# Where the score scatters are issued in a two-layer graph kernel: held back around each batch's features

## The chip, the cores and the metric

The kernel runs on one core of one Trainium2 chip. The metric is the device time of one execution in microseconds (us); for a kernel, the median of several runs. TensorE is written PE, VectorE DVE, ScalarE ACT, GpSimd POOL and SyncE SP, as the profile does. Each engine works through a queue of its own in the order in which the program was written down, and waits on semaphores.

## What is computed

Inputs are `x` (16 batches x 1024 nodes x 256) and one 1024 x 1024 matrix `adj` that is mostly zero (the edge lists below have room for 135 x 128 entries). Two graph layers follow each other for every batch:

```python
# layer 0
feats  = x @ W1.T;  f1 = feats @ W2 + b2
coefs  = softmax(leaky_relu(f1[:, None] + f1[None, :]) + adj)
h      = coefs @ feats + bias2 + x
# layer 1
S      = sigmoid(relu(h[u] @ W1u + h[v] @ W1v + b1) @ W2 + b2)   # for each pair u, v
a      = (S * adj).T @ h
m      = (adj @ h) * h
z      = beta1*h + beta2*(a @ Wa + ba) + beta3*(m @ Wm + bm)
```

`S` is multiplied by `adj`, so it matters only where `adj` has an edge.

## The kernel before

**Layer 0, batch by batch.** For each of 16 batches PE makes the features from the turned `x` (`begin_features`, four steps of 4 matmuls each, L991), then the row of f (`begin_f`: eight transposes at L965), and then attention in eight chunks (`attention(b, c)`, 8 matmuls of 128 x 257 each, L1041); each matmul of these two lines shows as two instructions in the profile. The features and the row of f of batch b + 1 are written down right after attention chunk 7 of batch b. Each features step needs one of two PSUM buffers of pool `p2`. It is emptied by DVE, which clips two columns (L1004, tile `f`), and then by ACT, which takes their exponential (L1008) and scales the features with it (L1016); only after that may PE fill the buffer again. Two further chains end at the same spot: attention's rows are divided and added by DVE (`keep_h`, L1052 and L1055), and the row of f is reduced by DVE (L973) and turned into `row` and `col` by ACT (L979, L980, L984), from which DVE spreads the weights of the next attention (L1028).

**Layer 1, edge by edge.** After attention, `h` is projected to both ends of an edge (`end`, L1079) and stored to memory. The scores are made on lists of edges, for three groups of batches together (5, 5 and 6 batches). A list has 135 slots for each group; a slot is 128 edges, and one slot is one *round*. In a round
- POOL fetches the far ends for the slot three rounds ahead (`fetch`, an indirect DMA, L1200 into tile `gv`, one of five buffers) and in every eighth round or so the near ends too (L1193, tile `gu`),
- DVE takes the maximum and minimum of the two ends (`compare`, two instructions of L1229),
- ACT adds up, one instruction pair for each batch of the group (`sums`, L1243); in a quarter of the last group's rounds DVE does it instead (L1240),
- after 16 rounds (a *part*) ACT applies tanh (`gates`, L1251), DVE adds one (L1270), and the part's 16 results are appended to the list `late` as 16 *scatters*: indirect DMAs of POOL, one for each slot (L1209, `sa_d<-lg,idx_s`).

The scatters are not issued at once. At the start of each round, behind its fetch, the function `first` takes one of them from `late`, or two when more than 12 stand there (`PARTS[0] - 4`). What is left at the end of the last group is issued together. Fetches and scatters stand in one queue, POOL's, in the order written down.

**What sets the order.** A `Timetable` holds entries of a planned time and a function; `run()` sorts them by time and calls them, so the planned time decides the order on every engine's queue and nothing else. `times.now` is moved along by PE's planned work. The rounds of a group are spread evenly between two planned times by `scores(g, start, end, ...)`: a round every 3.67 us in the first group (planned 391 to 879), 3.47 in the second (883 to 1348) and 3.86 in the third (1351 to 1868). `scores` is called when the whole loop over the batches has been written down. Rounds of the first two groups therefore lie beside layer 0 of batches 5 to 15, the third beside the products and `gather` of groups already scored (L1139, L1159, L1344); there ACT and DVE prepare the gathers' weights (tile `apart`, L1326 and L1331) from `sat`, loaded by SP.

Of the kernel before, what the change touches and what calls it, by code (L numbers as in the profile page):

```python
# [371 lines left out]
def edge_layers(  # L372
# [59 lines left out]
    first = first_stack.enter_context(tc.tile_pool(name="first", bufs=1, side="right"))  # L432
# [750 lines left out]
    PARTS = [16, 32, 48, 64, 80, 96, 112, 124, 131, len(SLOTS)]  # L1183
    AHEAD = GV - 2
    HA = 9
    SA = 7
    late = []

    def fetch(g, k):
        t, s = SLOTS[k]  # L1190
        if s == 0:
            gu = st["gu", t] = pools["gath", g].tile([P, SIZE[g] * R], F32, name="gu", bufs=2)
            nc.gpsimd.indirect_dma_start(  # L1193
                out=gu,
                out_offset=None,
                in_=pu_d[g],
                in_offset=bass.IndirectOffsetOnAxis(ap=key_u[:, t : t + 1], axis=0),
            )
        gv = st["gv", k] = pools["gath", g].tile([P, SIZE[g] * R], F32, name="gv", bufs=GV)
        nc.gpsimd.indirect_dma_start(  # L1200
            out=gv,
            out_offset=None,
            in_=pw_d[g],
            in_offset=bass.IndirectOffsetOnAxis(ap=idx_v[:, t, s : s + 1], axis=0),
        )

    def scatter(g, lg, i, k):
        t, s = SLOTS[k]
        dma = nc.gpsimd.indirect_dma_start(  # L1209
            out=sa_d[g],  # L1210
            out_offset=bass.IndirectOffsetOnAxis(ap=idx_s[:, t, s : s + 1], axis=0),
            in_=lg[:, i, : SIZE[g]],
            in_offset=None,
            bounds_check=N * N - 1,
            oob_is_err=False,
        )
        tc.declare_no_dep(dma.ins, group=f"sa{g}", reason="edges of their own")
        tc.add_to_no_dep_group(f"sa{g}", dma.ins)
# [12 lines left out]
    def place_of(k):  # L1231

        part = next(i for i, end in enumerate(PARTS) if k < end)
        return (PARTS[part - 1] if part else 0), PARTS[part]
# [18 lines left out]
    def scores(g, start, end, on_vector):  # L1253

        for k in range(len(SLOTS)):
            time = start + k * (end - start) / len(SLOTS)

            def first(k=k):
                for n in range(AHEAD) if k == 0 else ():
                    fetch(g, n)  # L1260
                if k + AHEAD < len(SLOTS):
                    fetch(g, k + AHEAD)
                for _ in range(min(len(late), 2 if len(late) > PARTS[0] - 4 else 1)):
                    late.pop(0)()

            def last(k=k):
                k0, k1 = place_of(k)
                lg = st["lg", k0]
                part = lg[:, : k1 - k0, : SIZE[g]]
                nc.vector.tensor_scalar(part, part, 1.0, None, ALU.add)  # L1270
                late.extend(lambda i=i: scatter(g, lg, i, k0 + i) for i in range(k1 - k0))

            times.at(time - (15.0 if k == 0 else 0.0), first)
            times.at(time + 0.1, lambda k=k: compare(k, 0))
            times.at(time + 0.9, lambda k=k: compare(k, 1))
            k0, k1 = place_of(k)
            if k == k0:
                times.at(time + 0.2, lambda k0=k0: st.update({("lg", k0): st["lg"]}))
            summed = lambda js, k=k, k0=k0: sums(k, js, st["lg", k0])
            if on_vector(k):  # L1280
                times.at(time + 1.7, lambda f=summed: f(range(SIZE[g])))
            else:
                for j in range(SIZE[g]):
                    times.at(time + 2.0 + 0.6 * j, lambda f=summed, j=j: f((j,)))
            if k + 1 == k1:
                times.at(time + 5.4, lambda k=k, k0=k0: gates(g, k, st["lg", k0]))
                times.at(time + 6.0, last)
        ended = end + 4.0
        if g + 1 == NG:
            times.at(ended, lambda: [late.pop(0)() for _ in range(len(late))])  # L1290
        return ended
# [118 lines left out]
    def attention(b, c):  # L1410
        end = times.matmuls(C * (D + 1), lambda: attend(b, c))
        times.at(end + 0.6, lambda: keep_h(b, c))
# [29 lines left out]
    times = Timetable()  # L1442
# [23 lines left out]
    for b in range(B):  # L1466
        at_once = b > 0 and b - 1 not in LATER
        more = b + 1 < B

        if b:  # L1470
            weigh_ends(b - 1, 2)
            one_end(b - 1, 2, 1)
            if at_once:
                messages(b - 1, 0, 0)
            one_end(b - 1, 3, 0)
            one_end(b - 1, 3, 1)
            weigh_ends(b - 1, 3)
            if b - 1 in LATER:
                times.at(times.now, lambda b=b: put_off(b - 1))
            if any(b == lo for lo, _ in GROUPS):  # L1480
                started.append(times.now + 19.0)
        attention(b, 0)
        if b == 0:
            grows(6, 7)
        if at_once:
            messages(b - 1, 0, 1)
        attention(b, 1)
        spreads(b, 0)
        if more:
            times.at(times.now, lambda b=b: load_x(b + 1))  # L1490
        if at_once:
            products(b - 1, 0, 1)
        if b == 0:
            for i in range(2):
                for h in range(H):
                    times.matmuls(2 * R, lambda i=i, h=h: sort_columns(i, h))
            times.matmuls(2 * R, sort_bias)
        attention(b, 2)
        if at_once:
            messages(b - 1, 1, 0)  # L1500
        turned_ends(b, 0)
        attention(b, 3)
        spreads(b, 1)
        if at_once:
            messages(b - 1, 1, 1)
        both_ends(b, 0)
        attention(b, 4)
        if at_once:
            products(b - 1, 2, 3)
        if not more:  # L1510
            times.at(times.now, lambda: take_up(LATER[0]))
            times.at(times.now + 20.0, lambda: take_up(LATER[1]))
        turned_ends(b, 1)
        if more:
            begin(b + 1, 0)
        attention(b, 5)
        both_ends(b, 1)
        if more:
            begin(b + 1, 1)
        attention(b, 6)  # L1520
        turned_ends(b, 2)
        attention(b, 7)
        for c2 in range(C // 2):
            if more:
                begin_features(b + 1, c2)
        one_end(b, 2, 0)
        turned_ends(b, 3)
        if more:
            begin_f(b + 1)
# [58 lines left out]
    b = B - 1  # L1588
    for n in range(3):
# [4 lines left out]
        time = products(b, 2, 3)  # L1594
        b = LATER[n]
# [31 lines left out]
    for i, at in starts.items():  # L1627
        if i == 5:
            continue
        b = LATER[i]  # L1630
# [53 lines left out]
    for n, (g, c) in enumerate((g, c) for g in order for c in range(C)):  # L1684
# [4 lines left out]
        else:  # L1689
            k, c1 = divmod(n - HA, C)  # L1690
# [77 lines left out]
```

## Time and profile before

| what | value |
|---|---|
| median of 3 runs | 2165.57 us (2164.74 to 2166.67) |
| the profiled execution's own time | 2166.46 us |
| its span, first to last instruction | 2164.4 us |
| PE busy | 2054.0 us (95%) |
| DVE, ACT, POOL busy | 1565.5, 1378.6, 1128.4 us |
| scatters L1209 | 405, 496.1 us of POOL |
| fetches L1200 | 405, 481.1 us of POOL |
| granted clock of PE, mean | 0.985 |
| first fetch and first scatter begin | 376.8 and 454.8 us |
| last scatter issued, last group's gathers follow | 1975.2 us |

All of it is one execution; times in the views count from its first instruction, and 2.06 us of its 2166.46 lie outside the span. Busy time is an engine's own. "Idle before, releaser" is the time an engine stood still before an instruction, and what ended it; the releaser "remote" is one that the trace does not name, and "issue" is time for which it shows no wait.

### The profile page before, as it was taken

Reading aid. Unit: us, or ns where it says so; the run is one execution under the profiler, and the core shown is the slowest. Engines: PE = TensorE matmul, PEld = TensorE weight load, DVE = VectorE, ACT = ScalarE, POOL = GpSimd, SP = SyncE. Lnnn points to the kernel's source line nnn. Section 1 sums busy time; section 2 is a strip of 40 time slices with the busy share of each in tenths; the row PEclk is TensorE's granted clock in tenths of the full one; section 3 lists DMA queues with packets and bytes.
Section 4 is the critical chain, followed back from the end, with each engine's and each line's share of the span. In section 5 each row is a group of like instructions: output and inputs, shape, how many; then the busy total and the mean of one; then the engine's idle time right before and its main releaser. Section 6 shows DMA issues by size and latency. Waiting matters only on the chain.

```text
span 2164.4 us, 28928 instructions
## 1 busy us (share of the span) xinstructions
PE 2054.0 (95%) x8566; PEld 1561.6 (72%) x8566; DVE 1565.5 (72%) x2316; ACT 1378.6 (64%) x4842; POOL 1128.4 (52%) x986
## 2 busy tenths in 40 slices
PE   6999999999999999989899899999999999999998
PEld 5887888777676767667678777456666767667887
DVE  6798875577767676667667776577888978885544
ACT  4212222476767767576777787468888788885554
POOL 2121221267666676667666668665767666674000
PEclk8999999999999999999999999999999999999999
DMA  6587776788877787788888889899999999997774
GB/s 211 201 328 292 287 294 249 257 267 274 282 260 256 262 277 249 270 282 268 267 298 283 270 276 341 310 344 413 392 388 384 402 410 385 368 396 276 266 240 134
DMA packets 248007, 644.37 MB, mean 298 GB/s; under 512 B 37154, under 2 KB 137506, under 8 KB 245794
## 3 DMA queue, kind: packets, MB, share of 16 engines
q0 software_dynamic: 82528, 349.79, 46.4%
q1 hardware_dynamic: 129474, 258.44, 32.5%
q10 hardware_dynamic: 35840, 34.22, 4.6%
q8 instruction: 69, 1.13, 0.2%
q14 instruction: 96, 0.79, 0.1%
HBM read 479.56 MB, written 162.92 MB: 297 GB/s over the span
## 4 chain that ended last, share of the span: by engine, by line
PE 56%; DVE 15%; issue 9%; DMA 7%; ACT 7%; POOL 3%; another core or an unknown queue 2%; ACTq 0%; POOLq 0%; DVEq 0%
PE pv L1041 16%; PE pm L1139 10%; PE pp L1079 9%; PE pzg L1344 7%; DVE gv L1229 6%; DMA gv<-pw_d,idx_v 6%; ACT gv L1243 4%; PE pea L1107 4%; PE pf L991 3%; PE pzh L1344 3%; PE pz L1159 2%; DVE apart L1331 2%; POOL sa_d L1209 2%; POOL gv L1200 1%
## 5 line engine op out<-in xcount | busy, mean ns | idle before, releaser
L1243 ACT ACTIVATE gv<-gv 128x272 f32<-128x272 f32 x2058 | 856.4, 419 | 301.5 <-DVE gv L1229 152.6
L1229 DVE TENSOR_TENSOR gv<-gv,gu 128x680 f32<-128x680 f32 (+1 forms) x810 | 705.5, 907 | 106.3 <-DMA gv<-pw_d,idx_v 101.4
L1200 POOL DMA_INDIRECT gv<-pw_d,idx_v x405 | 481.1, 1188 | 386.3 <-ACT gv L1243 248.6
L1209 POOL DMA_INDIRECT sa_d<-lg,idx_s x405 | 496.1, 1225 | 131.5 <-issue 112.5
L1041 PE MATMUL pv<-feats,eT 128*128 128x257 f32 x2048 | 468.6, 381 | 5.1 <-DVE eT L1028 3.5
L1139 PE MATMUL pm<-adj_sb,xh 128*128 128x512 f32 x1024 | 450.0, 592 | 1.8 <-DVE xh L1055 1.8
L1041 PEld LDWEIGHTS pv<-feats,eT 128*128 128x128 f32 x2048 | 382.0, 190 | 67.6 <-DVE eT L1028 9.6
L1344 PE MATMUL pzg<-ha_g,apart 128*128 128x256 f32 x1536 | 370.5, 384 | 25.0 <-DVE apart L1331 18.3
L1243 ACT ACTIVATION_READ_ACCUMULATOR gv<-gv 128x1 f32 x2058 | 389.2, 189 | 0.0
L1344 PEld LDWEIGHTS pzg<-ha_g,apart 128*128 128x128 f32 x1536 | 287.7, 190 | 91.2 <-DVE apart L1331 35.6
L1139 PEld LDWEIGHTS pm<-adj_sb,xh 128*128 128x128 f32 x1024 | 193.1, 190 | 220.0 <-issue 217.2
L1326 ACT COPY apart<-sat 128x640 f32<-128x640 f32 (+1 forms) x192 | 264.4, 1391 | 87.8 <-PE pzh L1344 46.7
L1079 PE MATMUL pp<-wuv,hT 128*128 128x272 f32 x1024 | 257.9, 402 | 20.6 <-ACT end L1093 7.1
L1331 DVE TENSOR_TENSOR apart<-apart,adj_sb 128x640 f32<-128x640 f32 (+1 forms) x192 | 165.9, 866 | 118.0 <-ACT apart L1326 112.5
L1079 PEld LDWEIGHTS pp<-wuv,hT 128*128 128x128 f32 x1024 | 196.4, 194 | 75.6 <-ACT end L1093 10.4
L1028 DVE SCALAR_TENSOR_TENSOR eT<-row,col,grown 128x512 f32<-128x512 f32 x256 | 183.1, 745 | 28.0 <-ACT col L984 25.1
L843 POOL DMA_INDIRECT table_d<-rec,at x52 | 57.5, 1106 | 267.2 <-DVE rec L836 160.4
L991 PE MATMUL pf<-w1T,xT 128*128 128x257 f32 x512 | 128.6, 405 | 30.6 <-ACT feats L1016 25.5
L1072 ACT COPY hT<-ph 128x512 f32<-128x512 f32 x96 | 55.2, 576 | 147.8 <-PE ph L1061 90.3
L991 PEld LDWEIGHTS pf<-w1T,xT 128*128 128x128 f32 x512 | 101.5, 202 | 54.5 <-ACT feats L1016 32.9
L1159 PE MATMUL pz<-wm,mT 128*128 128x256 f32 x512 | 118.1, 384 | 6.0 <-DVE mT L1150 5.3
L1107 PE MATMUL pea<-wa,hT 128*128 128x256 f32 x512 | 122.3, 382 | 0.0
(184 smaller groups left out, 1616.2 us busy)
## 6 DMA issues: line engine op xcount, KB each, us to landing
sa_d<-zero SPq DMA_DIRECT2D x128, 512.0 KB
sat<-sa_d SPq DMA_DIRECT2D x128, 320.0 KB
sat<-sa_d SPq DMA_DIRECT2D x64, 384.0 KB
pu_d<-end SPq DMA_DIRECT2D x64, 272.0 KB
pw_d<-end SPq DMA_DIRECT2D x64, 272.0 KB
xh<-in_x_dram SPq DMA_DIRECT2D x16, 1024.0 KB
ha_d<-ea SPq DMA_DIRECT2D x64, 256.0 KB
zb_d<-zb ACTq DMA_DIRECT2D x64, 256.0 KB
```

What stands on the lines that cost most here:

```text
L991: nc.tensor.matmul(pf[:, i, : D + 1], lhsT=st["xT"][:, h, c * P : (c + 1) * P], rhs=w1T[:, h, :], start=(h == 0), stop=(h == H - 1),)
L1041: nc.tensor.matmul(pv[:, : D + 1], lhsT=st["eT", b, k, j // 4][:, j % 4, i * P : (i + 1) * P], rhs=st["feats", b][:, j, :], start=(j == 0) ...
L1079: nc.tensor.matmul(pp[:, k, :R], lhsT=st["hTi", b, i][:, h, k * P : (k + 1) * P], rhs=wuv[:, side, h, :], start=(h == 0), stop=(h == H - 1),)
L1107: nc.tensor.matmul(pp[:, k, :], lhsT=st["hTi", b, i][:, h, k * P : (k + 1) * P], rhs=wa[:, h, :], start=(h == 0), stop=(h == H - 1),)
L1139: nc.tensor.matmul(pm, lhsT=held[b][:, c, h * P : (h + 1) * P], rhs=adj_sb[:, c, span], start=(c == 0), stop=(c == C - 1),)
L1200: nc.gpsimd.indirect_dma_start(out=gv, out_offset=None, in_=pw_d[g], in_offset=bass.IndirectOffsetOnAxis(ap=idx_v[:, t, s : s + 1], axis=0),)
L1209: dma = nc.gpsimd.indirect_dma_start(out=sa_d[g], out_offset=bass.IndirectOffsetOnAxis(ap=idx_s[:, t, s : s + 1], axis=0), in_=lg[:, i, : ...
L1229: nc.vector.tensor_tensor(mv, mv, mu, op)
L1243: nc.scalar.activation(one[:, j, :], one[:, j, :], AF.Copy, accum_out=lg[:, i, j : j + 1])
L1326: nc.scalar.copy(apart.rearrange("p g v -> p v g"), sat)
L1331: nc.vector.tensor_tensor(apart, apart, a.unsqueeze(1).to_broadcast([P, SIZE[g], P]), ALU.mult)
L1344: nc.tensor.matmul(st["pzg", g, vc][j // 4][:, j % 4, :], lhsT=apart[:, j, :], rhs=ha, start=(c == 0 and j % 2 == 0), stop=(c == C - 1 and ...
```

## The change

Each batch gets a *calm* window in planned time, from 6 us before the planned end of its attention chunk 7 to 13 us after it. A round whose planned time lies in such a window still fetches, but takes no scatter from `late`. In the other rounds two are taken when more than 8 stand in the list, where it was more than 12. Nothing else changes: the same 405 scatters, the same fetches, no new buffer and no new wait.

```diff
     late = []
+    calm = []
+
+    def take(n):
+        for _ in range(min(len(late), n)):
+            late.pop(0)()
...
-            def first(k=k):
+            def first(k=k, rest=any(a <= time < b for a, b in calm)):
                 for n in range(AHEAD) if k == 0 else ():
                     fetch(g, n)
                 if k + AHEAD < len(SLOTS):
                     fetch(g, k + AHEAD)
-                for _ in range(min(len(late), 2 if len(late) > PARTS[0] - 4 else 1)):
-                    late.pop(0)()
+                if not rest:
+                    take(2 if len(late) > PARTS[0] - 8 else 1)
...
         attention(b, 7)
+        calm.append((times.now - 6.0, times.now + 13.0))
         for c2 in range(C // 2):
```

## The prediction

> **What bounds the kernel now.** I read the busy shares first, then the windows (busy time of each engine in a stretch), then what ended the idle time.
>
> ```profile
> PE 2054.0 (95%) x8566; PEld 1561.6 (72%) x8566; DVE 1565.5 (72%) x2316; ACT 1378.6 (64%) x4842; POOL 1128.4 (52%) x986
> ```
>
> PE is the bound. The change removes no work of PE, so only PE's idle time can move. In the two stretches in which scatters run, the columns after the length are PE, PEld, DVE, ACT, POOL busy, granted clock, DMA share, GB/s:
>
> ```profile
> 454.00:1340.00 886.00, 835.80 (x3514) 641.58 (x3513) 640.82 (x1019) 635.75 (x2644) 596.32 (x508) 0.98 0.83 274
> 1340.00:1980.00 640.00, 610.27 (x2245) 412.02 (x2243) 494.44 (x582) 501.53 (x1773) 434.39 (x343) 0.99 0.97 371
> ```
>
> PE idles 886.00 - 835.80 = 50.2 us in the first (groups one and two of the rounds) and 640.00 - 610.27 = 29.7 us in the second (the third group). Those 80 us are all that is at stake. Next the windows from the end of attention chunk 7 to the last transpose of the row of f: batch 5 without a scatter, then batches 9, 10 and 11, and the sum over batches 5 to 14.
>
> ```profile
> 444.81:455.30 10.49, 10.41 (x53) 8.69 (x53) 5.68 (x15) 9.32 (x38) 3.17 (x4) 1.00 0.57 175
> 839.84:855.48 15.64, 12.00 (x54) 9.95 (x53) 5.95 (x15) 11.21 (x49) 9.10 (x9) 0.89 0.75 247
> 949.60:961.43 11.83, 10.67 (x54) 8.61 (x53) 8.17 (x19) 11.19 (x48) 3.99 (x4) 1.00 0.73 241
> 1047.90:1066.67 18.77, 12.41 (x53) 10.23 (x53) 11.41 (x23) 12.56 (x52) 12.30 (x12) 0.82 0.82 255
> sum 144.24, PE 115.39 PEld 93.93 DVE 83.18 ACT 112.82 POOL 74.03; mean PE 11.54 PEld 9.39 DVE 8.32 ACT 11.28 POOL 7.40
> ```
>
> The same work takes 10.5 us in one batch and 18.8 in another. Batches 3 and 4, before any round, take 10.8 and 10.4 (10.6 on average). The ten stretches thus exceed ten quiet ones by 144.24 - 106 = 38.2 us, 28.85 of them idle PE (144.24 - 115.39), the rest slower matmuls at a granted clock of 0.82 to 0.90. The excess by batch: b6 0.5, b7 4.7, b8 3.5, b9 5.0, b10 1.2, b11 8.2, b12 7.8, b13 5.9, b14 1.5. So 28.85 of the first window's 50.2 us idle lie here and 21.3 elsewhere.
>
> What ends the wait in b11 is seen on PE, DVE and POOL in order of time:
>
> ```profile
> 1047.74 3.64 PE L991 MATMUL pf<-w1T,xT 128*128 128x257 f32 x16
> 1057.73 0.79 PE L991 MATMUL pf<-w1T,xT 128*128 128x257 f32 x1 [6.36 <-ACT feats L1016]
> ```
>
> ```profile
> 1056.41 0.16 DVE L1004 TENSOR_SCALAR f<-pf 128x2 f32<-128x2 f32 x1 [2.02 <-remote]
> ```
>
> ```profile
> 1053.38 1.29 POOL L1209 DMA_INDIRECT sa_d<-lg,idx_s  x1 [0.30 <-issue]
> 1054.98 0.96 POOL L1200 DMA_INDIRECT gv<-pw_d,idx_v  x1 [0.30 <-issue]
> 1056.25 1.01 POOL L1209 DMA_INDIRECT sa_d<-lg,idx_s  x1 [0.30 <-issue]
> ```
>
> PE filled both buffers by 1051.4. The clip L1004 that empties them started at 1056.4, released by something the trace doesn't name, five microseconds after the matmuls it reads. Meanwhile POOL went from fetch to scatter without a pause. Going through all late releases of this kind, none lies before the first scatter (454.8), and 26 of 27 begin while POOL has issued without a pause for 7 us or more, a state it is in for 72% of that time. Whether the full POOL queue makes the report late, or both have one cause, the trace doesn't say.
>
> **Term one, the features.** The code's planned times put 59 rounds into calm windows; 45 of them issued scatters, 55 in all. Planned time trails real time by 5 us (b5) to 49 (b15), but the rounds drift along with it: the fetches of the calm rounds run from 4 us before the real end of chunk 7 to 16 after. The windows do hit the stretches. There POOL falls from scatter and fetch in turn, (1182 + 300) + (1176 + 300) = 3.0 us of a round's 3.7, to 1.5 us (durations from the rows below, 0.3 the issue gap above). Does that free PE? For: b10, with one scatter at the start and two late, takes 11.83. Against: b8 and b13 had no scatter in the first ten microseconds and still idled 3.5 and 4.3 us; in b7, b8 and b13 the lateness begins about 4 us before chunk 7's end, where scatters are still issued. That leaves b9, b11, b12, b14: 5.0 + 8.2 + 7.8 + 1.5 = 22.5 us. Bounds 0 and -22.5 (-38 if all went). With evidence on both sides I take half: **-11**.
>
> **Term two, rounds beside layer 0 (groups one and two).** What is withheld comes back as doubled rounds, since two are taken from nine entries up instead of thirteen. Counted from the planned order, rounds with 0, 1 and 2 scatters go from 61, 296, 48 to 120, 175, 110.
>
> ```profile
> L1209 POOL DMA_INDIRECT sa_d<-lg,idx_s x238 | 281.3, 1182 | 75.3 <-issue 66.4 <-DVE lg L1270 1.9 <-DVE inv L1052 1.9
> L1200 POOL DMA_INDIRECT gv<-pw_d,idx_v x236 | 277.5, 1176 | 206.4 <-ACT gv L1243 130.7 <-issue 46.2 <-ACT feats L1008 16.4
> L1193 POOL DMA_INDIRECT gu<-pu_d,key_u x34 | 39.1, 1150 | 11.1 <-issue 8.8 <-DMA xh<-in_x_dram 1.0 <-DVE gv L1229 0.6
> ```
>
> A round measures 886 / 237 = 3.74 us (474 compares, two to a round). With a fetch, 0, 1 or 2 scatters and an eighth of the near fetch, POOL needs 1.7, 3.1 or 4.6 us. A doubled round exceeds the pitch by 0.9 us, and four to six in a row delay the last fetch by 4 to 5 us; three rounds of lead (11 us) cover that only partly. What waits is DVE's compare, then ACT's sums and whatever of layer 0 is queued on both behind them:
>
> ```profile
> DVE gv L1229 <- DMA gv<-pw_d,idx_v: 44.4, 15, 7.9
> ```
>
> I went through these 15 waits and counted how many scatters the new order puts ahead of each fetch, 1.48 us each. Fewer stand ahead of six (-19.8 us at most), more ahead of five that already wait (+10.4). What reaches PE is at most the 21.3 us of idle outside the features over 44.4 = 0.48. Bounds: -4.5 for all, +5 if only the worse ones count. Half of -4.5: **-2**.
>
> **Term three, the third group.** It has no calm window, only the lower threshold, so it pays without a gain.
>
> ```profile
> DVE gv L1229 <- DMA gv<-pw_d,idx_v: 57.0, 31, 5.3
> ```
>
> Seven of these fetches get two or three more scatters ahead, 18 queue places x 1.48 = 26.8 us; times 29.7 / 57.0 = 0.52 that is +13.9 on PE. At a DMA share of 0.97 the landing may hang on the transfer engines and not on POOL's order, which would make it 0. Half: **+7**.
>
> **Edits at nothing.** Reading the flag and `take` issue the same instructions. Backlog stays at 18 entries at most and no buffer is reused sooner. SP loads the first group's scattered scores (`sat`) only from 1463 us, over 500 us after its last scatter. The last flush falls from 13 scatters to 10, but PE has work without a gap from about 1980 to the end, so nothing is gained.
>
> **Sum.** -11 - 2 + 7 = -6. The profiled execution took 2166.46 us (span 2164.4 and 2.06 outside); so 2160.5. It stands 0.9 above the median of 2165.57, so **2160** (2159.6).
>
> **Two rules that speak against this.** The row: scatters cost POOL 1182 ns and 0.3 us of gap. The Trainium skill, "DMA: Bandwidth & Descriptors", section "Anatomy of one DMA — SWDGE (gpsimd) path", says that most of a transfer's fixed two microseconds is the receipt of the write and that making descriptors is small; by it, moving scatters would move nothing, and the sum would be 2166. The rows of POOL show the issue itself to be long. The other row: PE's buffers were released late only while POOL issued without a pause. The Trainium skill, "SBUF — State Buffer", section "SBUF: two separate sides", says that engine and transfer ports cannot contend and that PE and ACT never wait on anyone; by it the first term would be nothing and the sum 2166.5 - 2 + 7 = 2171.
>
> **Rivals.**
> *Nothing moves* (2166): late reports have another cause, which b8 and b13 speak for, and the waits cancel. Against: b5 and b10.
> *Slower, by doubled rounds*: POOL's 4.6 us against a pitch of 3.7 delays fetches in slots 5 to 9 of each part of sixteen, where the waits already cluster, and the features win nothing. Price: 0 + 5 + 13.9 = 18.9, at most 2184.5; half of it 2175. It decides from the point where the fetch waits of the third group grow by more than twice what the features win, as about half passes on to PE. Against: a scatter moved is never a scatter added, and POOL is 68% busy there (434.39 of 640).
> *The change doesn't do what it says*: planned windows miss the real stretches (2166 or a little more). The drift above speaks against it.
>
> **Chances.** Forecast 0.45, nothing 0.22, slower 0.29, misses 0.04. A measurement can tell about 0.2% (4.3 us) from no change; so faster 0.45, same 0.26, slower 0.29. The forecast's own range goes from -22.5 - 4.5 = -27 to about -4, 2139 to 2161. Reaching to the slower case until two in ten is left out gives 2140 to 2178.
>
> **What would show it.** Right: stretches of b9, b11, b12 near 11 to 13 us, their sum near 133 (144 now), PE's idle from 454 to the end of layer 0 down from 50 to about 37, and 7 us more PE idle in the third group, with longer waits of L1229 there. Wrong in term one: stretches as long as now with POOL half empty. Wrong in term three: waits of L1229 after 1340 at 57 us or less. What I fear most is that late reports follow the doubled rounds to where they now fall, into chunks 1 to 6 of attention, which show as idle time of PE at L1041.

## The result and the profile after

The changed kernel is slower: 2210.8 us (median of 6 runs, 2194.2 to 2215.5) against 2159.3 for the kernel before (6 runs; the three made beside the changed kernel took 2146.6 to 2153.8). The ratio is 1.023, with a 95% interval of 1.020 to 1.026. Forecast were 2160 us and a range of 2140 to 2178.

The profiled execution of the changed kernel is its fastest, 2194.2 us with a span of 2192.1, so 27.7 us over the span of before. The busy shares of its page, to be held against the first line shown of before:

```profile
PE 2063.5 (94%) x8566; PEld 1562.7 (71%) x8566; DVE 1566.7 (71%) x2316; ACT 1377.8 (63%) x4842; POOL 1121.9 (51%) x986
```

Same instructions; PE is busy 9.5 us longer (its matmuls ran at a lower granted clock) and idle 18.2 us longer (2192.1 - 2063.5 = 128.6 against 2164.4 - 2054.0 = 110.4). Next the windows of the feature stretches (end of attention chunk 7 to the last transpose of the row of f) of batches 5, 9, 10 and 11, and the sum over batches 5 to 14, columns as before:

```profile
446.82:457.30 10.48, 10.40 (x53) 8.68 (x53) 5.68 (x15) 9.32 (x38) 2.67 (x3) 1.00 0.61 183
850.11:862.35 12.24, 10.45 (x54) 8.61 (x53) 5.82 (x14) 9.74 (x41) 4.55 (x5) 1.00 0.93 322
964.24:975.02 10.78, 10.59 (x53) 8.62 (x53) 7.22 (x18) 10.53 (x45) 2.55 (x3) 1.00 0.79 291
1068.31:1079.07 10.76, 10.57 (x53) 8.60 (x53) 6.71 (x16) 10.63 (x47) 4.46 (x5) 1.00 0.91 306
sum 117.15, PE 109.00 PEld 88.88 DVE 72.97 ACT 103.57 POOL 36.60; mean PE 10.90 PEld 8.89 DVE 7.30 ACT 10.36 POOL 3.66
```

Batch 11 needs 10.8 us instead of 18.8, all ten 117.15 instead of 144.24: the stretches won 27.1 us, with POOL at half its former load. So the change did there what it says. The rest of the kernel gave more back. Cut at the same instructions (end of chunk 7, last transpose), the two profiled executions differ as follows:

| part | before | after | difference |
|---|---|---|---|
| up to the end of chunk 7 of batch 5 | 444.8 | 446.8 | +2.0 |
| feature stretches, batches 5 to 14 | 144.2 | 117.2 | -27.1 |
| between them, up to the end of chunk 7 of batch 15 | 742.9 | 784.0 | +41.1 |
| from there to the end | 832.4 | 844.2 | +11.8 |

In the part between the stretches PE's idle time went from 21.4 to 49.9 us; the remaining 12.6 of the 41.1 are slower matmuls. What DVE waits for, after, from 454 to 1340 and from 1340 to 1980 us (before: 44.4 us in 15 waits and 57.0 in 31):

```profile
DVE gv L1234 <- DMA gv<-pw_d,idx_v: 88.1, 32, 11.9
```

```profile
DVE gv L1234 <- DMA gv<-pw_d,idx_v: 84.4, 42, 12.3
```

In both parts the waits for fetches grew in size and above all in number: 32 where there were 15, 42 where there were 31. Over the whole execution DVE's waits for fetches went from 101.4 to 167.7 us. A second kind of wait is that of DVE and ACT for "remote". Most of these are on matmuls that the trace ended some microseconds earlier; I call them late reports of PE. They fell in all, from 108.6 to 73.2 us, and in the feature stretches from 15.6 us to none. One of the waits for fetches can be followed in the timeline, first POOL:

```profile
1099.97 2.55 POOL L1214 DMA_INDIRECT sa_d<-lg,idx_s  x1 [0.30 <-issue]
1102.83 1.07 POOL L1205 DMA_INDIRECT gv<-pw_d,idx_v  x1 [0.30 <-issue]
1104.20 1.13 POOL L1214 DMA_INDIRECT sa_d<-lg,idx_s  x1 [0.30 <-issue]
1105.63 1.35 POOL L1214 DMA_INDIRECT sa_d<-lg,idx_s  x1 [0.30 <-issue]
1107.29 0.98 POOL L1205 DMA_INDIRECT gv<-pw_d,idx_v  x1 [0.30 <-issue]
1108.58 1.14 POOL L1214 DMA_INDIRECT sa_d<-lg,idx_s  x1 [0.30 <-issue]
1110.02 1.25 POOL L1214 DMA_INDIRECT sa_d<-lg,idx_s  x1 [0.30 <-issue]
1111.57 0.99 POOL L1198 DMA_INDIRECT gu<-pu_d,key_u  x1 [0.30 <-issue]
1112.87 0.97 POOL L1205 DMA_INDIRECT gv<-pw_d,idx_v  x1 [0.30 <-issue]
```

then DVE and PE:

```profile
1113.06 0.87 DVE L1234 TENSOR_TENSOR gv<-gv,gu 128x680 f32<-128x680 f32 x1 [1.87 <-DMA gv<-pw_d,idx_v]
...
1120.49 1.64 DVE L1234 TENSOR_TENSOR gv<-gv,gu 128x680 f32<-128x680 f32 x2 [5.19 <-DMA gv<-pw_d,idx_v]
1126.12 0.17 DVE L1052 RECIPROCAL inv<-pv 128x1 f32<-128x1 f32 x1 [3.98 <-remote]
...
1131.09 0.72 DVE L1091 TENSOR_TENSOR end<-pp,bu 128x544 f32<-128x544 f32 x1 [3.51 <-remote]
```

```profile
1121.91 1.89 PE L1107 MATMUL pea<-wa,hT 128*128 128x256 f32 x8
1131.88 1.97 PE L946 MATMUL pt<-ident,xh 128*128 128x128 f32 x8 [8.07 <-DVE end L1091]
```

A calm window has just passed. POOL catches up with two scatters between any two fetches, the round with the near fetch among them; its fetch goes out at 1112.9 and DVE stands 5.2 us before it has landed. Then DVE stands twice more for "remote", reports of PE on matmuls that the trace ended by 1122.1, and PE stands 8.1 us. Both kinds of loss are here: fetches that come late, and late reports of PE. The latter lay mostly outside the features before, too (93 of the 108.6 us).

### The profile page after: what moved, and what is told of

Read it like the earlier page. It is cut to its first block, busy times and chain, and to the rows that moved or that the text cites. A ratio compares the mean times of both kernels' runs of the same rounds, so it can differ in the third digit from the quotient of the medians.

```text
span 2192.1 us, 28946 instructions
## 1 busy us (share of the span) xinstructions
PE 2063.5 (94%) x8566; PEld 1562.7 (71%) x8566; DVE 1566.7 (71%) x2316; ACT 1377.8 (63%) x4842; POOL 1121.9 (51%) x986
## 4 chain that ended last, share of the span: by engine, by line
PE 53%; DVE 17%; issue 10%; ACT 9%; DMA 8%; POOL 2%; another core or an unknown queue 1%; POOLq 0%; ACTq 0%; DVEq 0%; SPq 0%
PE pv L1041 14%; PE pm L1139 9%; PE pp L1079 8%; PE pzg L1349 8%; DVE gv L1234 7%; DMA gv<-pw_d,idx_v 6%; ACT gv L1248 5%; PE pea L1107 4%; PE pzh L1349 3%; PE pf L991 2%; PE pz L1159 2%; ACT apart L1331 2%; DVE apart L1336 1%; POOL sa_d L1214 1%
## 5 line engine op out<-in xcount | busy, mean ns | idle before, releaser
L1234 DVE TENSOR_TENSOR gv<-gv,gu 128x680 f32<-128x680 f32 (+1 forms) x810 | 707.6, 908 | 191.9 <-DMA gv<-pw_d,idx_v 167.7
L1205 POOL DMA_INDIRECT gv<-pw_d,idx_v x405 | 470.6, 1162 | 411.2 <-ACT gv L1248 271.4
L1214 POOL DMA_INDIRECT sa_d<-lg,idx_s x405 | 505.6, 1248 | 136.9 <-issue 112.0
L1041 PE MATMUL pv<-feats,eT 128*128 128x257 f32 x2048 | 476.5, 384 | 11.5 <-issue 5.9
L1139 PE MATMUL pm<-adj_sb,xh 128*128 128x512 f32 x1024 | 457.4, 598 | 15.7 <-issue 9.4
L991 PE MATMUL pf<-w1T,xT 128*128 128x257 f32 x512 | 122.7, 393 | 11.0 <-ACT feats L1016 10.0
```

Of the source, the lines that this page charges most:

```text
L991: nc.tensor.matmul(pf[:, i, : D + 1], lhsT=st["xT"][:, h, c * P : (c + 1) * P], rhs=w1T[:, h, :], start=(h == 0), stop=(h == H - 1),)
L1041: nc.tensor.matmul(pv[:, : D + 1], lhsT=st["eT", b, k, j // 4][:, j % 4, i * P : (i + 1) * P], rhs=st["feats", b][:, j, :], start=(j == 0) ...
L1139: nc.tensor.matmul(pm, lhsT=held[b][:, c, h * P : (h + 1) * P], rhs=adj_sb[:, c, span], start=(c == 0), stop=(c == C - 1),)
L1205: nc.gpsimd.indirect_dma_start(out=gv, out_offset=None, in_=pw_d[g], in_offset=bass.IndirectOffsetOnAxis(ap=idx_v[:, t, s : s + 1], axis=0),)
L1214: dma = nc.gpsimd.indirect_dma_start(out=sa_d[g], out_offset=bass.IndirectOffsetOnAxis(ap=idx_s[:, t, s : s + 1], axis=0), in_=lg[:, i, : ...
L1234: nc.vector.tensor_tensor(mv, mv, mu, op)
```

## The experiments

Four sets of four and one of two ran, each set on a chip of its own, with runs of the kernel before beside it. These took 2112 to 2114 us beside the first two sets and the last, 2144 beside the third, 2163 beside the fourth. So each kernel below is compared with the runs of before beside it, and stages are compared within a kind: "quiet" names the sets at 2112 to 2114, in whose traces no engine ever waited for "remote". The edits are cut short ("..." marks what is left out) and stand against the changed kernel, or against the kernel before where the text says so. Where scatters are left out, scores are missing from the output; these kernels measure a cost and are no candidates.

My theory after the first result (1): the price comes from the doubled rounds, which hold up fetches. Rivals: the time won in the features is given back by rounds that bind anyway (2); holding back costs by itself (3).

**The lower threshold alone**

```diff
-        calm.append((times.now - 6.0, times.now + 13.0))
```

> No calm windows; two scatters are taken when more than 8 stand in the list. Counted from the planned order, rounds with two scatters are 95, in runs of up to four (before: 48 in runs of up to two; after: 110 in runs of up to five). Theory 1, the loss comes from runs of doubled rounds, which delay fetches and make PE late outside the features: most of the loss of the changed kernel and none of its gain, 40 to 50 us slower than before, ten feature stretches together as long as before (about 144 us). Theory 2, the rounds bind whatever the scatters do and the time won in the features is only given back: within 5 us of before. Theory 3, the holding back itself costs (the empty rounds): within 5 us of before.

Measured: 2135.9 against 2112.4 us, ratio 1.012 (1.010 to 1.013). That is half of the 45 us that the changed kernel loses in the other quiet set (below). The features took 116.3 us, against 107.2 in a quiet profile of before. Nothing is withheld here: the threshold alone brings the same scatters closer together, and that alone costs 24 us.

**The calm windows alone**

```diff
-                    take(2 if len(late) > PARTS[0] - 8 else 1)
+                    take(2 if len(late) > PARTS[0] - 4 else 1)
```

> Calm windows as in the changed kernel, two scatters only when more than 12 stand in the list, as before. Doubled rounds are 77, of them 18 in the third group as before (17). Theory 1 (runs of doubled rounds): the features win 25 to 27 us as in the changed kernel, 29 more doubled rounds instead of 62 cost about 29/62 of 53 = 25 us, together within 10 us of before, third group as before. Theory 2 (given back): as the changed kernel, at least 20 us slower. Theory 3 (holding back costs): nearly the whole loss of the changed kernel, 20 to 40 us slower.

Measured: 2138.3 us, ratio 1.012 (1.011 to 1.014), +26. The features took 123.7 us, more than the 107.2 of the quiet profile of before: no gain at all.

**Calm windows whose scatters are left out**

```diff
-                if not rest:
-                    take(2 if len(late) > PARTS[0] - 8 else 1)
+                n = 2 if len(late) > PARTS[0] - 4 else 1
+                if rest:
+                    del late[:n]
+                else:
+                    take(n)
```

> Calm windows; the scatters that the kernel before would have issued in calm rounds are left out altogether, so some edges' scores are missing from the output; all else as before, the doubled rounds among it. Theory 1 (the price is the catching up): the gain of the features stands alone, 20 to 30 us faster than before. Theory 2 (the time won is given back in attention): within 8 us of before, stretches short and the rest longer. Theory 3 (holding back costs): slower than before.

Measured: 2113.1 us, ratio 1.001 (0.9995 to 1.002). This kernel issues 350 scatters, 55 fewer. It differs from the run above in the withheld scatters alone, so issuing those 55 later costs 25 us. Theory 3 falls as the main cause; that holding back is quite free isn't shown, since 55 fewer scatters may hide a few microseconds of it. And the gain that I expected isn't there.

**Calm windows, doubled rounds kept apart**

```diff
-                    take(2 if len(late) > PARTS[0] - 8 else 1)
+                    two = len(late) > PARTS[0] - 8 and not doubled[-1] and not near(k)
+                    doubled.append(two)
+                    take(2 if two else 1)
...
```

> Calm windows and the threshold of the changed kernel, but no two doubled rounds in a row, and none with a near fetch (tile gu). Doubled rounds 84, all single. POOL then needs at most 4.6 + 3.1 us in two rounds of 7.4. Theory 1, runs of doubled rounds: the features keep 20 to 27 us, the price falls to 5 to 15, so 5 to 20 us faster than before. If every doubled round costs, however placed: 84 - 48 = 36 more, 36/62 of 53 = 31 us, no gain or up to 10 slower. Theory 2: 20 us slower or more.

Measured: 2143.7 us, ratio 1.015 (1.013 to 1.017), +31. Keeping the doubles apart doesn't bring the gain back: 5 to 20 us faster was expected of theory 1, and 31 slower is what the other reading said, that a doubled round costs however it is placed. (One wait of 11.6 us of PE at the start of the second group's gathers is part of it.)

The absent gain called for a profile of before in such a set.

**The kernel before, once more.** No edit.

> The kernel before, once more with a profile, because the runs beside the first four experiments took 2112 us where the profiled one took 2166, and no engine waited for an unnamed releaser in those four traces. If the late reports of PE belong to the chip or to that stretch of time and not to the order of the scatters: about 2112 us, features of batches 5 to 14 near 110 us instead of 144, no wait for an unnamed releaser. If they belong to the order of before: features near 144 us again and such waits again.

Measured: 2112.0 us. Features of batches 5 to 14: 107.2 us, no "remote". Its windows for batches 11 and 14, scatters in them as ever (POOL 8.4 and 8.6 us):

```profile
1028.64:1039.14 10.50, 10.37 (x54) 8.75 (x53) 6.07 (x15) 9.74 (x41) 8.37 (x8) 1.00 0.81 241
1221.36:1232.29 10.93, 10.68 (x54) 8.61 (x53) 7.44 (x17) 10.15 (x45) 8.58 (x8) 1.00 0.78 253
```

So the order of before doesn't cost the features anything as such: the 38 us of excess that I built term one on came together with the late reports, and those with the chip, or with the time of the run. What scatters in a stretch do where there are late reports, a quiet set can't tell.

**The changed kernel, once more.** No edit.

> The changed kernel, once more beside the runs of before. Theory 1 (every doubled round costs, by a late fetch; 62 more of them): without late reports there is nothing to win in the features, so slower by the sum of the two parts measured alone or less: 25 to 45 us over before. If the first result came from the late reports moving to other places: within 10 us of before where no such reports occur.

Measured: 2159.5 against 2114.1 us, ratio 1.022 (1.019 to 1.024), so the same loss without a single late report. The same two stretches, now without scatters:

```profile
1044.45:1061.00 16.55, 13.18 (x54) 10.74 (x53) 10.01 (x22) 12.17 (x51) 5.49 (x5) 0.79 0.79 254
1251.81:1267.08 15.27, 11.94 (x53) 9.90 (x53) 10.42 (x23) 12.83 (x54) 5.35 (x6) 0.89 0.82 289
```

POOL is emptier and the stretch longer. DVE ahead of the first of them shows why:

```profile
1038.58 1.64 DVE L1234 TENSOR_TENSOR gv<-gv,gu 128x680 f32<-128x680 f32 x2 [3.65 <-DMA gv<-pw_d,idx_v]
1040.15 1.22 DVE L955 COPY xT<-pt 128x1024 f32<-128x1024 f32 x1
1041.28 0.68 DVE L959 TENSOR_TENSOR xh<-xh,bias_bc 128x512 f32<-128x512 f32 x1
1043.18 0.94 DVE L1234 TENSOR_TENSOR gv<-gv,gu 128x680 f32<-128x680 f32 x1 [1.22 <-DMA gv<-pw_d,idx_v]
...
1049.36 0.15 DVE L1004 TENSOR_SCALAR f<-pf 128x2 f32<-128x2 f32 x1
```

DVE lost 4.9 us to two late fetches, so it reaches the clip L1004 at 1049.4 though PE had filled the buffers by 1047.9; PE idles 3.4 us and the granted clock of the stretch falls to 0.79. The waits of DVE, before and after, from 454 to 1340 us:

```profile
DVE gv L1229 <- DMA gv<-pw_d,idx_v: 50.4, 18, 8.6
```

```profile
DVE gv L1234 <- DMA gv<-pw_d,idx_v: 113.8, 45, 11.4
```

Up to the end of chunk 7 of batch 15, features went from 107.2 to 129.4 us and the rest from 731.0 to 743.3, together +34.5: 23.4 of it PE idle, 11.1 slower matmuls. After it +15.7. So 63 us more waiting on DVE became 34.5 on the path.

Are the fetches issued later, or do they land more slowly? The traces have both, taking as the landing the last update of the fetch's semaphore. For the rounds from 454 to 1340 us of the quiet pair, a fetch lands 6.5 us after its issue in before and 6.4 in the changed kernel (medians), so the landing isn't slower. From the issue to the first compare there are 10.1 us before and 8.8 after, though more of these compares had to wait. In the pair of the result it is the same: landing 6.1 and 6.2 us, issue to compare 10.8 and 9.9. So POOL issues the fetches too late. And in before 56 of 250 compares began 0.3 to 2 us after their fetch had landed: just in time, and in no list of waits.

**The changed kernel, third group as before**

```diff
-                    take(2 if len(late) > PARTS[0] - 8 else 1)
+                    take(2 if len(late) > PARTS[0] - (4 if g + 1 == NG else 8) else 1)
```

> The changed kernel, but in the third group two are taken only from thirteen on, as before (16 doubled rounds there instead of 33). Theory 1: the third group gives back its share, 5 to 14 us less than the changed kernel, and its fetch waits fall to those of before. If the third group's waits hang on the transfer engines alone: as the changed kernel within 4 us.

Measured: 2153.0 us, 6.5 below the changed kernel beside it; from the end of batch 15's chunk 7 on 837.7 instead of 842.5 us, fetch waits there 63.2 instead of 80.4. Term three is real, and the threshold's own share is of the size that I gave it.

**Never two**

```diff
-        calm.append((times.now - 6.0, times.now + 13.0))
...
-                    take(2 if len(late) > PARTS[0] - 8 else 1)
+                    take(1)
```

> No calm windows and never two scatters in a round: 388 rounds with one, 17 scatters left for the end. Theory 1 (a doubled round delays a fetch): 48 doubled rounds fewer than before, each worth about 0.5 to 0.9 us, so 10 to 35 us faster than before, with fewer waits for fetches at slots 5 to 9 of each part. If doubles cost only where they come in fours: within 5 us of before.

Measured: 2128.7 us, ratio 1.008 (1.005 to 1.010). A miss: the 48 doubled rounds of before cost next to nothing. Up to the end of chunk 7 of batch 15 this kernel is 3 us faster than before; the part after it is 21 us longer, and in it PE stands 13.9 us in one place, where the second group's last scatters and the loads of its scores (`sat`) wait for each other. I take it that before's doubled rounds at the head of each part are covered because the rounds without a scatter at its end leave POOL time.

So it isn't every doubled round. I took as theory 4 POOL's capacity over a whole interval between windows: what is withheld must fit into fewer rounds, and POOL was busy for 644 of 886 us already in the quiet profile of before, and with 0.3 us of issue for each of its 538 instructions for 806, or 91%.

**The second scatter of each doubled round left out**

```diff
                 if not rest:
-                    take(2 if len(late) > PARTS[0] - 8 else 1)
+                    two = len(late) > PARTS[0] - 8
+                    take(1)
+                    if two:
+                        del late[:1]
```

> The changed kernel, with the second scatter of every doubled round left out altogether, so that some edges' scores are missing from the output; calm windows and all else as in it. Theory 1 (the price is the time that the returned scatters take on POOL's queue ahead of fetches): the price goes, within 6 us of before or faster. If the order alone, the holding back or the windows cost: still 20 us slower or more.

Measured: 2118.5 against 2144.3 us, ratio 0.987 (0.983 to 0.991). With the same windows and without the catching up the kernel is 26 us faster than before, in a set with some late reports (features 118.8 us). It issues 295 scatters instead of 405, so how much of the 26 us is the smaller number of scatters, and how much the order, it doesn't part.

**Calm windows up to batch 10, and from batch 11 on.** Two kernels, one with each condition.

```diff
-                    take(2 if len(late) > PARTS[0] - 8 else 1)
+                    take(2 if len(late) > PARTS[0] - 4 else 1)
...
-        calm.append((times.now - 6.0, times.now + 13.0))
+        if b <= 10:
+            calm.append((times.now - 6.0, times.now + 13.0))
...
+        if b >= 11:
+            calm.append((times.now - 6.0, times.now + 13.0))
```

> Calm windows for batches up to 10 alone, two scatters only from thirteen on, as before. Here windows lie 98 us apart: 26 rounds, 5 of them calm, so 21 rounds for 26 scatters. POOL needs 1.66 + 26/21 x 1.48 = 3.5 us in a round of 3.7. Theory 4, POOL's capacity: it just suffices, 0 to 6 us slower than before. Rival, every doubled round costs alike (12 more than before, at 26 us for 29 more when all batches are calm): 11 us slower.

> Calm windows for batches 11 to 15 alone, two scatters only from thirteen on. Here windows lie 64 us apart in planned time: 18 rounds, 5 or 6 of them calm, so 13 rounds for 18 scatters. POOL needs 1.66 + 18/13 x 1.48 = 3.7 us in a round planned at 3.5. Theory 4, POOL's capacity: it does not suffice, fetches fall behind, 18 to 26 us slower than before, the loss in the stretches of batches 11 to 14. Rival, every doubled round costs alike (17 more than before): 15 us slower or less, and about as much for each as in the other half.

Measured: +12.3 us (ratio 1.006, 1.003 to 1.010) and +18.6 (1.009, 1.006 to 1.013). The first is what the rival said and not 0 to 6; the second lies at the lower end of theory 4. Both fall into a set with late reports, which lengthen single stretches by 5 to 8 us, so this pair doesn't decide between the two.

**The near fetch four rounds earlier, in the kernel before**

```diff
+    def early_near(t, s):
+        if s == 0 and (t == 0 or WIDTHS[t - 1] < 7):
+            yield t
+        if s == 4 and WIDTHS[t] >= 7:
+            yield t + 1
...
-        if s == 0:
-            gu = st["gu", t] = ...
+        for near in early_near(t, s):
+            gu = st["gu", near] = ...
```

> The kernel before, with its own rule for scatters and no calm windows, but each near fetch (tile gu) is issued four rounds earlier, away from the far fetch that it is used with. In before the waits for fetches lie at every eighth slot, behind the round with the near fetch, 50 us in each of the two stretches. If what is late is the landing of two transfers issued one behind the other: the waits fall by a third to a half and PE wins 5 to 15 us. If POOL's total load is what counts: no change, within 4 us.

Measured: 2132.3 against 2144.3 us, ratio 0.994 (0.991 to 0.997), with fetch waits of 31.3 us from 454 to 1340 and 37.4 from 1340 to 1980, as expected if the landing of two transfers in a row is what is late. The edit moves 42 of the 63 near fetches, nearly all by four rounds; those of the narrow tiles stay.

**The kernel before, in the fourth set.** No edit.

> The kernel before once more with a profile, as the measure for the three others of this set, since its time was 2112 us beside eight of the runs, 2144 beside four, and 2147 to 2167 beside the first result. If late reports (waits for an unnamed releaser on what PE has done) are what sets those apart, this run shows them in proportion to its time over 2112: none at 2112, some 30 us of such waits at 2144, about 100 at 2165.

Measured: 2164.5 us, features 134.2, waits for "remote" on DVE and ACT 56.6 us in all. Late reports are back, but I had expected about 100 us of them, as in the first profile (108.6), which took nearly the same time: their sum doesn't follow the time closely.

**No scatters at all**

```diff
-                for _ in range(min(len(late), 2 if len(late) > PARTS[0] - 4 else 1)):
-                    late.pop(0)()
+                del late[:2]
...
```

> The kernel before without any scatter (no score reaches the output); POOL's fetches stay. It bounds what any placing of the scatters can win. Theory 4 (POOL's time ahead of the fetches is the price, and before has it covered): 0 to 15 us faster than before where no late reports occur. Where they occur: if a POOL that issues without a pause brings them on, they vanish and the time falls to about 2100 to 2112 whatever before takes; if they have nothing to do with POOL, they stay, and the gain is at most 15 us there too.

Measured: 2091.8 against 2163.0 us, ratio 0.967 (0.962 to 0.973). No late report is left, and all features together take 106.1 us. The stretch from 454 to 1340 us, before beside it and without scatters:

```profile
454.00:1340.00 886.00, 841.38 (x3549) 641.99 (x3548) 644.97 (x1026) 642.44 (x2680) 605.73 (x513) 0.99 0.84 279
```

```profile
454.00:1340.00 886.00, 876.16 (x3695) 663.87 (x3694) 674.34 (x1073) 676.81 (x2829) 355.49 (x295) 1.00 0.86 296
```

PE's idle falls from 44.6 to 9.8 us. On this chip, then, there are late reports only with scatters. Whether those in the feature stretch bring them on or those elsewhere, this run doesn't part.

**The changed kernel with the near fetch earlier.** The same edit as above, in the changed kernel.

> The changed kernel with each near fetch issued four rounds earlier; calm windows, threshold, 405 scatters as in it. If the price of the change is a landing that is late behind two fetches and two scatters in one round: more than half of it goes, 10 to 20 us slower than before instead of 45. If the price is POOL's total load in the rounds between the windows, which this doesn't lower: 30 us slower or more.

Measured: 2207.3 us, ratio 1.022 (1.016 to 1.028), +44. Its fetch waits, 454 to 1340 and 1340 to 1980 us:

```profile
DVE gv L1240 <- DMA gv<-pw_d,idx_v: 75.2, 37, 7.8
```

```profile
DVE gv L1240 <- DMA gv<-pw_d,idx_v: 35.0, 25, 4.0
```

110 us of waits for fetches in all, about as many as before has beside it (47.1 + 65.7 = 112.8), but 28 us more of them beside layer 0 and 31 less in the third group. The closest kernel to hold it against is the next one, the near fetch earlier without the change: 2149.9 us, with fetch waits of 25.0 and 34.6. Against that the change costs 57 us; the fetch waits beside layer 0 triple and those of the third group stay. Waits for "remote" make 89 us here, 72 there. So the price doesn't go with the near fetch, as the second half of the expectation said, and the late fetches are still the larger part of what grew. The feature stretches took 140.4 us, against 135.2 without the change.

**The near fetch earlier, again.** No further edit.

> The kernel before with the near fetch four rounds earlier, as in the earlier run that was 0.6% faster, here beside another run of before. If that gain is from shorter waits for fetches (31 and 37 us there): 5 to 15 us faster here too. If it only avoided late reports of PE: no change where before takes 2112.

Measured: 2149.9 us, ratio 0.994 (0.991 to 0.998). The gain holds: 0.6% in a second set. Its profile has waits for fetches of 59.6 us instead of 112.8, and for "remote" of 72.1 instead of 56.6, so the gain doesn't come from fewer late reports. In a quiet set it wasn't run.

**A gather in the place of each scatter**

```diff
-        dma = nc.gpsimd.indirect_dma_start(
-            out=sa_d[g], out_offset=IndirectOffsetOnAxis(ap=idx_s[...]), in_=lg[:, i, : SIZE[g]], ...
+        seen = dense.tile([P, MOST], F32, name="seen", bufs=12)
+        nc.gpsimd.indirect_dma_start(
+            out=seen[:, : SIZE[g]], in_=sa_d[g], in_offset=IndirectOffsetOnAxis(ap=idx_s[...]), ...
```

> The kernel before, but in the place of each scatter an indirect gather with the same 128 indices and the same 20 or 24 bytes each, from the scores' buffer in memory into a small tile that nothing reads (no score reaches the output). POOL then issues as densely as before, while nothing is scattered. If POOL's dense issue brings on the late reports of PE and the late fetches: the time of before within 10 us, with late reports wherever before has them. If the scattered writes do: the time without scatters, about 2092 us, and no late reports.

Measured: 2114.8 against 2111.8 us, ratio 1.002 (1.000 to 1.003). In a quiet set, then, the price of a scatter isn't the scattered write: a gather of the same size costs as much. What both have is the issue on POOL and a transfer of 128 small pieces; since fetches land no later after their issue with scatters (6.5 us) than without any (6.8, in the run without scatters), I put the price down to the issue. Whether that also holds for the late reports this run can't say, since the set had none.

**Every second scatter left out**

```diff
-                    late.pop(0)()
+                    kept.append(late.pop(0))
+                    if len(kept) % 2:
+                        kept[-1]()
```

> The kernel before with every second scatter left out (half of the scores missing from the output), 203 issued in all and at most one in a round. If the cost goes with the number of scatters: half way between the time without any (2092 us) and before. If it goes with long stretches in which POOL has no pause: nearly the time without scatters, 2092 to 2100 us, and hardly any late report.

Measured: 2093.6 against 2111.8 us, ratio 0.991 (0.989 to 0.994), with 209 scatters. The time without any scatter, in another set, was 2091.8: the first half of them is nearly free, the second costs 18 us. I read this as the bend of a queue that fills up, and the change as a push along it: no scatter more, but the same number in less time.

How full POOL was can be counted from its instructions: the time from 454 to 1340 us that it spent in stretches of over 40 us without a pause (under 0.45 us from one instruction to the next). In the quiet sets:

| kernel | us in such stretches | against before |
|---|---|---|
| every second scatter left out | 0 | -18 |
| scatters of calm rounds left out | 227 | +1 |
| a gather for each scatter | 268 | +3 |
| before | 318 | 0 |
| never two | 355 | +15 (13.9 of it one wait) |
| threshold alone | 413 | +24 |
| changed kernel | 534 | +45 |
| changed kernel, third group as before | 534 | +39 |
| calm alone | 576 | +26 |
| calm, doubles apart | 629 | +31 |

More time without a pause goes with more loss, though not in strict order; the count leaves out the third group, where the lower threshold acts too. It hangs on the limit, besides: over 60 us the threshold alone has none and before has 169. So it is a sign, not a proof. Nor is the loss for each doubled round added any steadier (0.5 us with the threshold alone, 0.7 in the changed kernel, 0.9 with the calm windows alone and with the doubles apart, and next to nothing for the 48 of before).

## Why the prediction was wrong

- **The bound** was right: PE, with only its idle time at stake. But the sum left out that idle PE also lowers the granted clock: 12.6 of the 41.1 us between the stretches, and 11.1 of the 34.5 without late reports, were slower matmuls. I had seen the clock in the rows (0.82 in batch 11) and priced it in the gain alone.
- **Term one** (-11 forecast, bounds 0 and -38): -27.1 in the profile of the result, beyond what I took and past the -22.5 that I had counted. That it went the right way there was partly luck: no other pair of profiles has it. In the quiet pair the change made the stretches 22 us longer, and in the fourth set, with the near fetch earlier, 5 us longer in spite of late reports. Its cause was half right. Late reports need scatters (without them none, and 71 us less), and in emptied stretches they nearly vanished (15.6 us to none, 10.9 to 1.5). But scatters in a stretch don't make it long by themselves: in a quiet set the stretches take 107 us with them.
- **Term two** (-2 forecast, bounds -4.5 and +5) is the step that failed: the part that it stands for grew by 41.1 us. I counted only the 15 waits that the trace of before showed, and how the new order moves each. Fetches that had just been in time weren't in that list, and they are where the loss came from: 32 waits instead of 15, and 45 instead of 18 in the quiet pair, where 56 compares of before had come within 2 us of waiting. I had the load of one round (1.7, 3.1 or 4.6 us against 3.7) but never summed it over the interval from one window to the next. From the rows shown that sum is quick, up to batch 10: 26 rounds, 5 calm, so 26 scatters in 21 rounds, 1.66 + 26/21 x 1.48 = 3.5 us of 3.7; from batch 11 on 18 scatters in 13 rounds, 3.7 us of 3.5 planned. By this estimate POOL hardly catches up before the next window, and later not at all. The two runs with half of the windows, which were to show it, didn't decide (12 us of loss where the sum just suffices); and the threshold alone, which withholds nothing, lost 24 us. What is shown is that the same scatters, closer together, make POOL issue the fetches later (10.1 us ahead of their use before, 8.8 after); how long a stretch POOL can bear isn't.
- **What is late next.** I named it as the thing to fear, late reports that follow the doubled rounds into attention; it happened (8.1 us of PE at L946 in batch 12). It should have been a term, though not the largest: over the whole execution late reports fell by 35 us while waits for fetches grew by 66.
- **Term three** (+7): +11.8 in the profile of the result, +15.7 in the quiet pair, of which the third group's own threshold gives back 4.8 to 6.5. Right in kind, and about half of what was measured.
- **Edits at nothing**: the loads of `sat` from 1463 us that I took for the first group's are the second group's, whose gathers the kernel puts first. Its last scatter began at 1455.0, 8 us before and not 500. In the change this cost nothing that shows, but where scatters drag on, it does: 13.9 and 11.6 us of PE in two of the runs.
- **The rival** of doubled rounds came closest: scatters in a row that delay fetches. But doubled rounds set apart still cost 31 us, and the 48 of before cost next to nothing, so neither the row of them nor their number alone is the price. It was priced with the same short list of waits, so 2184.5 was too low an upper end. Its condition (waits in the third group up by more than twice what the features win) held in the quiet pair, where they won nothing, but not in the pair of the result: +27 us of waits against 27 won, and slower all the same. The loss was decided beside layer 0, which the condition left out.
- **The two rules** that I weighed: the page "DMA: Bandwidth & Descriptors" of the Trainium skill (section "Anatomy of one DMA — SWDGE (gpsimd) path") would have had moving scatters move nothing, since making descriptors is small; moving them cost 2.2 to 2.3%, and the run with gathers in their place, the one with half of them and the times of issue and landing point to the issue on POOL as the price. By "SBUF — State Buffer", section "SBUF: two separate sides", the first term would have been nothing; in the quiet pair there was indeed nothing to win, in the pair of the result 27 us. That rule speaks of ports; the late reports have no place in it.

Open stays why PE's reports are late beside some sets and not beside others, with the same program, and whether POOL's issue or the writes bring them on there. On the two calm halves of the batches the runs don't decide. A lead of four rounds for the fetches, with a sixth buffer of `gv`, wasn't tried.

## What to carry to other kernels

Work that is held back comes back: before moving it, sum the load of the engine that must do it over the whole time that is left, not for one round, and compare with what that time holds. (Here the sum would have warned; it wasn't shown to give the size.) A list of the waits that a trace shows bounds what can be won, not what can be lost; for the loss, count those that are just in time. Profile the kernel before more than once when a gain rests on single long stretches, since here 38 us of excess were there in one profile of the kernel before and absent in another.

## What the runs showed of the hardware that I had not expected

- The same program took 2112 to 2114 us in three sets and 2144 to 2163 in others (medians), with late reports of PE in the slower ones alone (a release 9 us after the recorded end of the matmul in the case shown, and later in a few others). Without scatters, in such a set, none was left and the time was 2092.
- All 405 scatters together cost 71 us in the set with late reports (2163.0 against 2091.8). In a quiet set 196 of them cost 18 (2111.8 against 2093.6). The landing of a fetch after its issue took 6.5 us with them and 6.8 without any.
- Moving 42 of the 468 indirect gathers up to four rounds ahead of their use made the kernel 0.6% faster (2132.3 against 2144.3, 2149.9 against 2163.0).
